# A graph layer whose loads move to ScalarE, with other buffers for gathered rows and sums

## The chip, the cores and the metric

The kernel runs on one core of a Trainium2 chip. The metric is the device time of one execution, in microseconds (us). PE is TensorE's matmul and PEld its weight load, DVE is VectorE, ACT ScalarE, POOL GpSimd and SP SyncE, which does no arithmetic and issues DMAs here. Each engine works through its own instructions in order; between engines, semaphores say when data is there or a buffer is free.

## What is computed

A layer of a graph network: 50,000 nodes of 160 features (64 scalars and 32 vectors of 3), 1,650,000 edges sorted by their destination `dst`, four numbers on each edge. For each edge the features of its source node are multiplied with the edge's numbers and with small weights; the results are summed over the edges of each destination; two more weights, a relu, the residual and a layer norm follow.

```python
e0, e1 = sh[:, 0:1], sh[:, 1:4]
dot  = einsum('eui,ei->eu', v[src], e1)
out0 = C0 * (s[src] * e0 @ W1 + dot * INV3 @ W2)
p3 = (s[src] @ W3)[:, :, None] * e1[:, None, :] * INV3
p4 = einsum('eui,uw->ewi', v[src] * e0[:, :, None], W4) * INV3
p5 = einsum('eui,uw->ewi', cross(v[src], e1[:, None, :]), W5) * INV6
out1 = C1 * (p3 + p4 + p5)
m_agg = segment_sum(concatenate([out0, out1]), dst)
h = concatenate([m_agg_s @ Ws * LIN_S, einsum('nui,uw->nwi', m_agg_v, Wv) * LIN_V])
x2 = x + relu(h)
result = layernorm(x + x2)
```

All of the weights are linear in the node's features, so the kernel sums first and multiplies after: for each of the four numbers k of an edge it sums (number k) × (source row of x) over the edges of a node, and multiplies the four sums of a node with matrices made of the weights.

## The kernel before

**Groups and pairs.** Edges are taken in units of 128, six units to a group (G = 6), two groups to a pair (PG = 2), twenty groups to a stretch of the tables (SG = 20, ten pairs). A group's destinations lie within a window of W = 32 nodes. There are 1,044 pairs, and 12,522 units.

**One pair.** `gather` (L345) issues twelve indirect DMAs on POOL (L349), each of 128 rows of x of 640 bytes, into one tile `xg` of [128, 12, 160] from a pool of four buffers. `spread` (L354) builds on DVE `hot`, which says for each edge which of the 32 nodes is its destination (L358), and `ha`, the same times the four numbers of the edge (L361). `group_sums` (L381) has PE multiply each unit's `ha` (128 edges × 4·32) with its gathered rows and sum the six units of a group in PSUM, in a tile `ps` of two groups from two buffers (L386; a matmul of float32 shows as two records). `turn_sums` (L394) has DVE transpose the pair's sums (L398) and add them into `ring` (L405) at a place that a register holds (`find`, L298).

**The order of the work.** The loop at L853 writes the order of all engines but POOL by hand: for pair p it asks for the gathers, then goes through the twelve units; after unit 1 comes the turning of pair p−1, after unit 3 the spreading of pair p+1, and after each unit `work(1.0)` (L748) takes tasks that are due, and a share of the steps of a pack. Tasks become due a number of pairs after or before some pair (`after_pair`, L741):

- of each block of 128 nodes whose last edges lie in pair p: `do_ahead` at p, which loads `xt` (the nodes' rows of x) for two blocks (L644); `do_block` at p+2, five matmuls of `ring` with the weights into `phb` (L704), then on DVE `y` and its statistics (L182 to L186); `do_root` at p+3, a square root on ACT (L191); `do_store` at p+4, L195 and L196 on DVE; `do_send` at p+6, the store of `o` (L784);
- of each stretch: `load` (L250) one stretch ahead; `cast` and `place` (L312), in which PE waits for `first` (L318) of DVE at L320, DVE makes the gathers' indices `si` and the places `rel`, and PE turns the edges' numbers into `pk` (L331);
- `ask_own` (L661) and `set_own` (L686), which bring in each node's own edge with two loads, `xr` and `sr`.

**Packs.** The edges of a node to itself lie among the others in the input. Sixteen packs (L463) take them out: a pack reads 128 rows of 790 edges (`read`, L471), copies and marks them (`begin`, ACT, L482 to L502), shifts the rest together with DVE (L559 to L566) and stores every row to `edges` and `selves` in HBM at an address that SP loads into a register (`store` and `put`, L594 to L619). It is a list of 77 steps, which the loop spreads evenly over the pairs that the pack has. The 17 store steps, of 16 DMAs each, follow each other.

**Queues.** `dq` (L247) is SP: the loads of `load`, of `read`, `xt`, `xr` and `sr`, the results and the packs' stores all stand in its one order. POOL has the gathers. ACT has the roots and the packs' copies.

**PSUM.** Eight banks: `bank` 1, `pk` 2, `marks` 1, `ps` 2, `phb` and the weights' products 2.

`wrote` (L374) tells the planner that a matmul needs no wait for the matmul that wrote the same buffer before, since that one's reader has been waited for.

Of the kernel before, what the change touches and what calls it, by code (L numbers as in the profile page):

```python
# [39 lines left out]
F32 = mybir.dt.float32  # L40
# [7 lines left out]
PSUM = bass.MemoryType.PSUM  # L48
# [54 lines left out]
def tile_gnn_resnorm(ctx: ExitStack, tc: tile.TileContext, x, src, dst, attr, W1, W2, W3, W4, W5, Ws, Wv, out, n_edges):  # L103
# [121 lines left out]
    last_of = [max(g for g in range(NG) if low[g] < (b + 1) * P) for b in range(nblocks)]  # L225

    with tc.tile_pool(name="once", bufs=1) as once, tc.tile_pool(name="raw", bufs=2) as rawp, \
            tc.tile_pool(name="idx", bufs=2) as idxp, tc.tile_pool(name="rows", bufs=4) as rowp, \
            tc.tile_pool(name="ops", bufs=3) as op, tc.tile_pool(name="sums", bufs=3) as sump, \
            tc.tile_pool(name="ring", bufs=2) as ringp, tc.tile_pool(name="node", bufs=3) as np_, \  # L230
            tc.tile_pool(name="ahead", bufs=4) as aheadp, tc.tile_pool(name="outs", bufs=3) as outp, \
            tc.tile_pool(name="psC", bufs=1, space=PSUM) as psC, tc.tile_pool(name="psK", bufs=2, space=PSUM) as psK, \
            tc.tile_pool(name="psP", bufs=1, space=PSUM) as psP, tc.tile_pool(name="psA", bufs=2, space=PSUM) as psA, \
            tc.tile_pool(name="psM", bufs=2, space=PSUM) as psM, ExitStack() as later_pools:

        spotp, ownp = (later_pools.enter_context(tc.tile_pool(name=name, bufs=bufs))
                       for name, bufs in (("spot", 3), ("own", 2)))
# [6 lines left out]
        slotsP = bank[:, 0, :]  # L244
        nc.vector.tensor_copy(slotsP, slots)

        dq = nc.sync  # L247
        begun = []

        def load(s):  # L250

            g0 = s * SG
            n = (min(NG, g0 + SG) - g0) * G
            if g0 >= NH:
                p0 = g0 * G * P - EH
                r6 = rawp.tile([P, P, 2 + NK], F32, name="r6")
                dq.dma_start(r6[:n].rearrange("u p c -> u (p c)"),
                             edges[0, p0 * (2 + NK):(p0 + n * P) * (2 + NK)].rearrange("(u q) -> u q", u=n))
                return s, n, None, r6[:n, :, 0], r6[:n, :, 1], r6[:n, :, 2:]
            e = slice(g0 * G * P, (g0 * G + n) * P)  # L260
            ri = rawp.tile([P, 2, P], I32, name="ri")
            ra = rawp.tile([P, P, NK], F32, name="ra")
            dq.dma_start(ri[:n, 0, :], src1[e].rearrange("(u p) o -> u (p o)", p=P))
            dq.dma_start(ri[:n, 1, :], dst1[e].rearrange("(u p) o -> u (p o)", p=P))
            dq.dma_start(ra[:n].rearrange("u p k -> u (p k)"), attr[e].rearrange("(u p) k -> u (p k)", p=P))
            return s, n, ri, None, None, ra[:n]

        def cast(loaded):
# [75 lines left out]

        def gather(placed, u, n):  # L345

            xg = rowp.tile([P, PG * G, D], F32, name="xg")
            for j in range(n):
                nc.gpsimd.indirect_dma_start(  # L349
                    out=xg[:, j, :], out_offset=None, in_=x,  # L350
                    in_offset=bass.IndirectOffsetOnAxis(ap=placed[0][:, u + j:u + j + 1], axis=0))
            return [xg[:, j, :] for j in range(n)]

        def spread(placed, u, n):  # L354

# [15 lines left out]
        def fresh(kind):  # L371
            written[kind].append([])

        def wrote(kind, ins):  # L374
            ws = written[kind]
            for old in ws[-3] if len(ws) > 2 else []:
                tc.declare_no_dep(ins.ins, old, reason="its reader has waited for it")
            ws[-1].append(ins.ins)
            return ins
# [83 lines left out]
        def pack(c):  # L463
# [7 lines left out]
            def read():  # L471
                T["pri"] = pri = packp.tile([P, 2, L + 1], I32, name="pri")
                T["pra"] = pra = packp.tile([P, LW, NK], F32, name="pra")
                dq.dma_start(pri[:n, 0, :L], src1[e].rearrange("(r e) o -> r (e o)", e=L))
                dq.dma_start(pri[:n, 1, :L], dst1[e].rearrange("(r e) o -> r (e o)", e=L))

                dq.dma_start(pri[:n, 1, L:], dst1[e0 + L:e0 + L + n * L].rearrange("(r e) o -> r (e o)", e=L)[:, 0:1])
                dq.dma_start(pra[:n, :L].rearrange("r e k -> r (e k)"), attr[e].rearrange("(r e) k -> r (e k)", e=L))

            def begin():  # L480
                T["prow"] = rows = packp.tile([P, L + 1, C], F32, name="prow")
# [142 lines left out]


            for head, j in [(False, j) for j in range(RS)] + [(True, 0)]:
                steps.append(partial(store, head, j))
            return steps + [stored]

        def rows_of(b):  # L630
# [8 lines left out]
        def ahead(bs):  # L639

            nb = rows_of(bs[0])[0]
            n0, n1 = rows_of(bs[0])[1].start, rows_of(bs[-1])[1].stop
            xt = aheadp.tile([P, BP, D], F32, name="xt")
            dq.dma_start(xt[:nb, :len(bs)], x[n0:n1, :].rearrange("(h n) d -> n h d", h=len(bs)))  # L644

            return [(xt[:, h],) for h in range(len(bs))]

# [13 lines left out]
        def ask_own(k, bs, got):  # L661

            n0, n1 = rows_of(bs[0])[1].start, rows_of(bs[-1])[1].stop
            assert rows_stored[0] == NR or row_start(rows_stored[0])[1][0] >= n1
            n = n1 - n0
            nq = next(q for q in range(math.ceil(n / W), n + 1) if n % q == 0)
            m = n // nq
            assert nq <= BP * P // W
            xr = ownp.tile([P, BP * P // W, D], F32, name="xr")
            sr = ownp.tile([P, BP * P // W], F32, name="sr")  # L670
            xs = x[n0:n1, :].rearrange("(w q) d -> w (q d)", q=nq).unsqueeze(0).to_broadcast([NK, m, nq * D])
            ss = selves[0, n0 * NK:n1 * NK].rearrange("(w q k) -> k w q", q=nq, k=NK)
            with nc.allow_non_contiguous_dma(reason="one number of each node"):
                if m == W:
                    dq.dma_start(xr[:, :nq].rearrange("p q d -> p (q d)"), xs)
                    dq.dma_start(sr[:, :nq], ss)
                else:
                    nc.vector.memset(xr[:, :nq], 0.0)
                    nc.vector.memset(sr[:, :nq], 0.0)
                    for k_ in range(NK):  # L680
                        r = slice(k_ * W, k_ * W + m)
                        dq.dma_start(xr[r, :nq].rearrange("p q d -> p (q d)"), xs[k_])
                        dq.dma_start(sr[r, :nq], ss[k_])
            got.extend((xr, sr, nq))

        def set_own(k, bs, got):  # L686
# [8 lines left out]
            if c0 + nq * W < c1:  # L695
                nc.vector.memset(ring[k][:, :, c0 + nq * W:c1], 0.0)

        def block(b, xt):
            nb, row = rows_of(b)
            k, c0 = b // SB, b % SB * P  # L700
            ph = psM.tile([P, D], F32, name="phb", tag="misc")
            fresh("misc")
            for i in range(ND):
                wrote("misc", nc.tensor.matmul(ph[:nb], ring[k][:, i, c0:c0 + nb], BWk[:, i, :],  # L704
                                               start=i == 0, stop=i == ND - 1))
                yield 1
            return norm1(np_, ph[:nb], xt[:nb], nb)
# [33 lines left out]
        def after_pair(p, f, *args):  # L741
            later.setdefault(p, []).append((f, args))
# [15 lines left out]
                else:  # L758
                    credit[0] -= cost

        of_nodes, resid, rstds, outs = {}, {}, {}, {}

        def do_ahead(b):
            bs = together(b)
# [1 line left out]
                of_nodes.update(zip(bs, ahead(bs)))  # L766

        def do_block(b):
            resid[b] = yield from block(b, *of_nodes.pop(b))

        def do_root(b):
            rstds[b] = norm2(np_, resid[b][1], rows_of(b)[0])
# [7 lines left out]
        def do_send(b):  # L780
            bs = together(b)
            if b == bs[-1]:
                n0, n1 = rows_of(bs[0])[1].start, rows_of(b)[1].stop
                dq.dma_start(out[n0:n1, :].rearrange("(h n) d -> n h d", h=len(bs)),  # L784
                             outs.pop(bs[0])[:rows_of(b)[0], :len(bs)])

        def do_cast(s):
# [57 lines left out]
                after_pair(p - 2, set_own, k, bs, got)  # L845
        for b, g in enumerate(last_of):
            p = g // PG
            after_pair(max(p, START - 1), do_ahead, b)
            for d, f in ((2, do_block), (3, do_root), (4, do_store), (6, do_send)):
                after_pair(p + d, f, b)  # L850
        later_pools.enter_context(tc.manual_schedule(engines={ET.SP, ET.PE, ET.DVE, ET.Activation}))
        turning = None
        for p, (s, g, ng) in enumerate(pairs):  # L853
# [8 lines left out]
                    after_pair(p + 8, read_flags)  # L862
            rows = gather(placed[s], (g - s * SG) * G, ng * G)
            for j, ps in enumerate(group_sums(p, rows, has.pop(p))):
                if j == 1 and turning:
                    turn_sums(*turning)
                    turning = None
                if j == 3 and p + 1 < len(pairs):
                    s1, g1, ng1 = pairs[p + 1]
                    has[p + 1] = spread(placed[s1], (g1 - s1 * SG) * G, ng1 * G)  # L870
                work(1.0)
                if packs and p >= START:
                    when = p + (j + 1) / (ng * G)
                    todo = math.ceil(len(packs[0]) * min(1, (when - began) / max(1, due[0] - began)))
                    for step in packs[0][done:todo]:
                        if step:
                            step()
                    done = max(done, todo)
                    if done == len(packs[0]):
                        packs.pop(0), due.pop(0)  # L880
                        done, began = 0, when
# [174 lines left out]
```

## Time and profile before

| | before |
|---|---|
| median of 3 runs | 17,993.06 us (17,989.49 to 18,003.85) |
| profiled execution | 18,022.17 us, span 18,020.0 us |
| mean granted TensorE clock | 0.625 |
| gathers | 12,522, of 0.949 us (median) |
| PE L386 | 25,044 records, 6,255 us |
| DVE `ha` L361 | 1,044 of 1.753 us, 1,830 us |
| SP stores of packs (L618) | 1,994 of 18.5 KB, 1,992 of 0.5 KB and 250 smaller |
| loads of `xt` / `xr` / results | 195 of 160 KB / 187 of 640 KB / 195 of 160 KB |
| moved by DMA | 1,337 MB, of these 1,027 MB by the gathers; 74 GB/s |

In a group's line of the page, "| busy, mean ns of one | idle before" follow the count. In a view of waits a line reads: who <- for whom: us in total, times, longest us; "issue" means that nothing in the profile ended the wait, "remote" that a semaphore did whose writer is not known. In an order of time a line begins with the start and the length in us, and the idle time of the engine before the instruction stands in brackets. A DMA that SP or ACT issues stands as SPq or ACTq, and its length is that of the issue.

### The profile page before, as it was taken

The page shows a single profiled execution, that of the slowest core. Times are in us where ns is not written, and L with a number is a line of the kernel's source. Part 1 is how long each engine was busy: PE and PEld are TensorE (multiplying, and loading weights), DVE is VectorE, ACT ScalarE, POOL GpSimd, SP SyncE. Part 2 cuts the span into 40 slices and gives each one's busy share as a digit, 9 for nine tenths or more (in the row PEclk, how much of TensorE's full clock was granted, in tenths as well). Part 3 has the DMA queues.
Part 4 walks back from the last instruction along what each step waited for, and adds up shares of the span by engine and source line. Part 5 has one row for each costly group of instructions (what it writes and reads, how often), then busy time and mean ns, then how long its engine had stood idle before and what let it go on. Part 6 is the DMA issues. An engine that isn't in the chain of part 4 may idle for free. (4 is left out here: it accounts for less than half of the span.)

```text
span 18020.0 us, 99721 instructions
## 1 busy us (share of the span) xinstructions
PE 6879.0 (38%) x29811; PEld 6014.7 (33%) x29812; DVE 7032.6 (39%) x11269; ACT 227.8 (1%) x479; POOL 12137.8 (67%) x12535
## 2 busy tenths in 40 slices
PE   3333334343333333333333333334333333333333
PEld 3333333333333333333333333333333333333333
DVE  4343443434434343443433434344343433434332
ACT  0000000000000000000000000000000000000000
POOL 6666666666666666666666666666666666666666
PEclk6666666666666666666666666666666666666666
DMA  2222323232232322323223232322323223232222
GB/s 71 74 69 72 80 71 81 69 82 72 73 79 70 83 71 73 79 69 81 72 72 79 70 79 72 82 69 72 80 70 82 69 73 80 69 79 72 73 72 63
DMA packets 961715, 1337.18 MB, mean 74 GB/s; under 512 B 411739, under 2 KB 716048, under 8 KB 957182
## 3 DMA queue, kind: packets, MB, share of 16 engines
q0 software_dynamic: 601056, 1026.60, 23.7%
q1 hardware_dynamic: 358674, 302.87, 6.1%
q8 instruction: 238, 3.90, 0.1%
q14 instruction: 307, 2.51, 0.0%
q10 hardware_dynamic: 1440, 1.29, 0.0%
HBM read 1258.50 MB, written 71.40 MB: 74 GB/s over the span
## 5 line engine op out<-in xcount | busy, mean ns | idle before, releaser
L349 POOL DMA_INDIRECT xg<-in_x,si x12522 | 12134.1, 969 | 5859.5 <-issue 3666.1
L386 PE MATMUL ps<-xg,ha 128*128 128x160 f32 x25044 | 6255.4, 383 | 9081.8 <-issue 8146.9
L386 PEld LDWEIGHTS ps<-xg,ha 128*128 128x128 f32 x25044 | 5171.1, 254 | 9859.0 <-issue 8902.6
L398 DVE STREAM_TRANSPOSE sums<-ps 128x320 f32<-128x320 f32 x1044 | 529.7, 507 | 6341.5 <-remote 4050.5
L361 DVE TENSOR_TENSOR ha<-hot,pk 128x1536 f32<-128x1536 f32 x1044 | 1830.2, 1753 | 35.8
L182 DVE SCALAR_TENSOR_TENSOR y<-phb,xt 128x160 f32<-128x160 f32 x391 | 125.6, 321 | 3508.3 <-PE ps L386 1623.2
L704 PE MATMUL phb<-BWk,ring 128*128 128x160 f32 (+1 forms) x3910 | 1181.7, 388 | 454.0 <-issue 452.9
L704 PEld LDWEIGHTS phb<-BWk,ring 128*128 128x128 f32 (+1 forms) x3910 | 925.6, 266 | 470.0 <-issue 469.5
L405 DVE TENSOR_TENSOR ring<-ring,sums 128x160 f32 x2087 | 683.1, 327 | 309.7 <-issue 224.2
L358 DVE TENSOR_TENSOR hot<-bank,rel 128x384 f32<-128x384 f32 x1044 | 572.4, 548 | 107.0 <-remote 70.5
L693 DVE STREAM_TRANSPOSE ring<-xr 128x1280 f32<-128x1280 f32 x188 | 466.1, 2479 | 6.5
L566 DVE COPY_PREDICATED prow<-marks,prow 128x2370 f32<-128x2370 int32 (+8 forms) x160 | 445.4, 2784 | 1.1
L320 PE MATMUL bank<-first,ones 120*128 120x20 f32 (+1 forms) x210 | 59.4, 365 | 815.1 <-DVE first L318 573.0
L320 PEld LDWEIGHTS bank<-first,ones 120*128 120x128 f32 (+1 forms) x210 | 49.8, 292 | 853.6 <-DVE first L318 597.5
L191 ACT ACTIVATE rstd<-mv,eps_t 128x1 f32<-128x1 f32 x391 | 115.2, 295 | 17061.4 <-DVE st L184 5415.1
L326 PE MATMUL bank<-ident,r 120*128 120x120 f32 x100 | 46.2, 462 | 703.1 <-issue 361.0
L566 DVE COPY_PREDICATED pra<-marks,pra 128x1580 f32<-128x1580 int32 (+8 forms) x160 | 306.5, 1915 | 0.0
L689 DVE TENSOR_TENSOR xr<-xr,sr 128x1280 f32<-128x1280 f32 x188 | 277.0, 1473 | 57.4 <-DMA sr<-selves 35.9
L326 PEld LDWEIGHTS bank<-ident,r 120*128 120x128 f32 x100 | 21.1, 211 | 727.4 <-issue 369.7
L196 DVE TENSOR_SCALAR o<-y,mv,rstd 128x160 f32<-128x160 f32 x391 | 146.1, 374 | 19.6 <-issue 3.7
L402 DVE TENSOR_TENSOR ring<-ring 128x1280 f32<-128x1280 f32 x97 | 143.0, 1474 | 1.8
L331 PE MATMUL pk<-ident,r 120*128 120x120 f32 (+1 forms) x400 | 139.5, 400 | 0.0
(349 smaller groups left out, 2156.2 us busy)
## 6 DMA issues: line engine op xcount, KB each, us to landing
xg<-in_x,si POOLq DMA_INDIRECT x12522
xr<-in_x SPq DMA_DIRECT2D x187, 640.0 KB
edges<-prow SPq DMA_DIRECT2D x1994, 18.5 KB
r<-edges SPq DMA_DIRECT2D x99, 360.0 KB
selves<-mine SPq DMA_DIRECT2D x1992, 0.5 KB
xt<-in_x SPq DMA_DIRECT2D x195, 160.0 KB
out<-o SPq DMA_DIRECT2D x195, 160.0 KB
pra<-in_attr SPq DMA_DIRECT2D x15, 1580.0 KB
```

Source lines behind the costliest of these rows:

```text
L196: nc.vector.tensor_scalar(o[:n], y[:n], mv[:n, 0:1], rstd[:n], op0=ALU.subtract, op1=ALU.mult)
L349: nc.gpsimd.indirect_dma_start(out=xg[:, j, :], out_offset=None, in_=x, in_offset=bass.IndirectOffsetOnAxis(ap=placed[0][:, u + j:u + j + ...
L358: nc.vector.tensor_tensor(hot[:, :n], slotsP[:, 0:W].unsqueeze(1).to_broadcast([P, n, W]), rel[:, u:u + n].unsqueeze(2).to_broadcast([P, n ...
L361: nc.vector.tensor_tensor(ha[:, :n], hot[:, :n].unsqueeze(2).to_broadcast([P, n, NK, W]), pk[:, :, u:u + n].rearrange("p k u -> p u k").un ...
L386: mm = nc.tensor.matmul(ps[:, j // G, :], ha[:, j].rearrange("p k w -> p (k w)"), xr, start=j % G == 0, stop=j % G == G - 1)
L398: nc.vector.transpose(at[:, :ng], ps[:, :ng].rearrange("p g (b f) -> p g b f", f=FB))
L402: nc.vector.tensor_tensor(ring[k][:, :, :TW - S], ring[k][:, :, :TW - S], ring[k - 1][:, :, S:], op=ALU.add)
L405: nc.vector.tensor_tensor(here, here, at[:, i], op=ALU.add)
L566: nc.vector.copy_predicated(what[:n, a:e], mi[:, r].unsqueeze(2).to_broadcast([n, e - a, what.shape[2]]), what[:n, a + d:e + d])
L689: nc.vector.tensor_tensor(xr[:, :nq], xr[:, :nq], sr[:, :nq].unsqueeze(2).to_broadcast([P, nq, D]), op=ALU.mult)
L693: nc.vector.transpose(ring[k][:, :, c0:c0 + nq * W].rearrange("p b (w q) -> p q b w", q=nq), xr[:, :nq].rearrange("p q (b f) -> p q b f", ...
L704: wrote("misc", nc.tensor.matmul(ph[:nb], ring[k][:, i, c0:c0 + nb], BWk[:, i, :], start=i == 0, stop=i == ND - 1))
```

## The change

- `loads` is ACT's queue. The loads of all stretches but the first, of the packs, `xt`, `xr` and `sr` and the stores of the results go through it; SP keeps the first stretch, the row table and the packs' stores.
- `do_ahead` comes three pairs earlier.
- Each store step of a pack is followed by two empty steps: 111 steps, not 77.
- Gathered rows lie in eight tiles of one group in place of four of two.
- `spread` of pair p+1 comes after unit 0, so before the turning of p−1.
- `ps` has three buffers; `phb` and the products have one, and `phb` holds the two blocks whose `xt` is loaded together. `wrote` looks back one buffer further for `ps` and no longer for the others.

```diff
-  rows: bufs=4            psA: bufs=2   psM: bufs=2
+  rows: bufs=4 * PG       psA: bufs=3   psM: bufs=1
-        dq = nc.sync
+        dq, loads = nc.sync, nc.scalar
...
         def load(s):
+            q = loads if s else dq
...
         def gather(placed, u, n):
-            xg = rowp.tile([P, PG * G, D], F32, name="xg")
+            rows = []
             for j in range(n):
+                if j % G == 0:
+                    xg = rowp.tile([P, G, D], F32, name="xg")
                 nc.gpsimd.indirect_dma_start(
-                    out=xg[:, j, :], out_offset=None, in_=x,
+                    out=xg[:, j % G, :], out_offset=None, in_=x,
...
         def wrote(kind, ins):
-            for old in ws[-3] if len(ws) > 2 else []:
+            for old in ws[-4] if kind == "ps" and len(ws) > 3 else []:
...
-                dq.dma_start(pri[:n, 0, :L], ...)
+                loads.dma_start(pri[:n, 0, :L], ...)
...
-                steps.append(partial(store, head, j))
+                steps += [partial(store, head, j), None, None]
...
-            dq.dma_start(xt[:nb, :len(bs)], ...)
+            loads.dma_start(xt[:nb, :len(bs)], ...)
...
-                    dq.dma_start(xr[:, :nq].rearrange("p q d -> p (q d)"), xs)
-                    dq.dma_start(sr[:, :nq], ss)
+                    loads.dma_start(xr[:, :nq].rearrange("p q d -> p (q d)"), xs)
+                    loads.dma_start(sr[:, :nq], ss)
...
-        def block(b, xt):
+        def block(b, xt, ph):
-            ph = psM.tile([P, D], F32, name="phb", tag="misc")
-            fresh("misc")
...
         def do_block(b):
-            resid[b] = yield from block(b, *of_nodes.pop(b))
+            bs = together(b)
+            if b == bs[0]:
+                sums_of[b] = psM.tile([P, BP, D], F32, name="phb", tag="misc")
+                fresh("misc")
+            resid[b] = yield from block(b, *of_nodes.pop(b), sums_of[bs[0]][:, b - bs[0]])
...
-                dq.dma_start(out[n0:n1, :].rearrange("(h n) d -> n h d", h=len(bs)),
+                loads.dma_start(out[n0:n1, :].rearrange("(h n) d -> n h d", h=len(bs)),
...
-            after_pair(max(p, START - 1), do_ahead, b)
+            after_pair(max(p - 3, START - 1), do_ahead, b)
...
             for j, ps in enumerate(group_sums(p, rows, has.pop(p))):
+                if j == 0 and p + 1 < len(pairs):
+                    s1, g1, ng1 = pairs[p + 1]
+                    has[p + 1] = spread(placed[s1], (g1 - s1 * SG) * G, ng1 * G)
                 if j == 1 and turning:
                     turn_sums(*turning)
                     turning = None
-                if j == 3 and p + 1 < len(pairs):
-                    s1, g1, ng1 = pairs[p + 1]
-                    has[p + 1] = spread(placed[s1], (g1 - s1 * SG) * G, ng1 * G)
```

More of the change, by code (lines that the diff above doesn't have):

```diff
@@ L227, in tile_gnn_resnorm @@
     with tc.tile_pool(name="once", bufs=1) as once, tc.tile_pool(name="raw", bufs=2) as rawp, \
-            tc.tile_pool(name="idx", bufs=2) as idxp, tc.tile_pool(name="rows", bufs=4) as rowp, \
+            tc.tile_pool(name="idx", bufs=2) as idxp, tc.tile_pool(name="rows", bufs=4 * PG) as rowp, \
             tc.tile_pool(name="ops", bufs=3) as op, tc.tile_pool(name="sums", bufs=3) as sump, \
@@ L232, in tile_gnn_resnorm @@
             tc.tile_pool(name="psC", bufs=1, space=PSUM) as psC, tc.tile_pool(name="psK", bufs=2, space=PSUM) as psK, \
-            tc.tile_pool(name="psP", bufs=1, space=PSUM) as psP, tc.tile_pool(name="psA", bufs=2, space=PSUM) as psA, \
-            tc.tile_pool(name="psM", bufs=2, space=PSUM) as psM, ExitStack() as later_pools:
+            tc.tile_pool(name="psP", bufs=1, space=PSUM) as psP, tc.tile_pool(name="psA", bufs=3, space=PSUM) as psA, \
+            tc.tile_pool(name="psM", bufs=1, space=PSUM) as psM, ExitStack() as later_pools:
         spotp, ownp = (later_pools.enter_context(tc.tile_pool(name=name, bufs=bufs))
@@ L256, in load @@
                 r6 = rawp.tile([P, P, 2 + NK], F32, name="r6")
-                dq.dma_start(r6[:n].rearrange("u p c -> u (p c)"),
+                q.dma_start(r6[:n].rearrange("u p c -> u (p c)"),
                              edges[0, p0 * (2 + NK):(p0 + n * P) * (2 + NK)].rearrange("(u q) -> u q", u=n))
@@ L262, in load @@
             ra = rawp.tile([P, P, NK], F32, name="ra")
-            dq.dma_start(ri[:n, 0, :], src1[e].rearrange("(u p) o -> u (p o)", p=P))
-            dq.dma_start(ri[:n, 1, :], dst1[e].rearrange("(u p) o -> u (p o)", p=P))
-            dq.dma_start(ra[:n].rearrange("u p k -> u (p k)"), attr[e].rearrange("(u p) k -> u (p k)", p=P))
+            q.dma_start(ri[:n, 0, :], src1[e].rearrange("(u p) o -> u (p o)", p=P))
+            q.dma_start(ri[:n, 1, :], dst1[e].rearrange("(u p) o -> u (p o)", p=P))
+            q.dma_start(ra[:n].rearrange("u p k -> u (p k)"), attr[e].rearrange("(u p) k -> u (p k)", p=P))
             return s, n, ri, None, None, ra[:n]
@@ L345, in gather @@
         def gather(placed, u, n):
-            xg = rowp.tile([P, PG * G, D], F32, name="xg")
+            rows = []
             for j in range(n):
+                if j % G == 0:
+                    xg = rowp.tile([P, G, D], F32, name="xg")
                 nc.gpsimd.indirect_dma_start(
-                    out=xg[:, j, :], out_offset=None, in_=x,
+                    out=xg[:, j % G, :], out_offset=None, in_=x,
                     in_offset=bass.IndirectOffsetOnAxis(ap=placed[0][:, u + j:u + j + 1], axis=0))
-            return [xg[:, j, :] for j in range(n)]
+                rows.append(xg[:, j % G, :])
+            return rows
         def spread(placed, u, n):
@@ L473, in read @@
                 T["pra"] = pra = packp.tile([P, LW, NK], F32, name="pra")
[L474 to L478, printed above, removed]
+                loads.dma_start(pri[:n, 0, :L], src1[e].rearrange("(r e) o -> r (e o)", e=L))
+                loads.dma_start(pri[:n, 1, :L], dst1[e].rearrange("(r e) o -> r (e o)", e=L))
+                loads.dma_start(pri[:n, 1, L:], dst1[e0 + L:e0 + L + n * L].rearrange("(r e) o -> r (e o)", e=L)[:, 0:1])
+                loads.dma_start(pra[:n, :L].rearrange("r e k -> r (e k)"), attr[e].rearrange("(r e) k -> r (e k)", e=L))
             def begin():
@@ L643, in ahead @@
             xt = aheadp.tile([P, BP, D], F32, name="xt")
-            dq.dma_start(xt[:nb, :len(bs)], x[n0:n1, :].rearrange("(h n) d -> n h d", h=len(bs)))
+            loads.dma_start(xt[:nb, :len(bs)], x[n0:n1, :].rearrange("(h n) d -> n h d", h=len(bs)))
             return [(xt[:, h],) for h in range(len(bs))]
@@ L681, in ask_own @@
                         r = slice(k_ * W, k_ * W + m)
-                        dq.dma_start(xr[r, :nq].rearrange("p q d -> p (q d)"), xs[k_])
-                        dq.dma_start(sr[r, :nq], ss[k_])
+                        loads.dma_start(xr[r, :nq].rearrange("p q d -> p (q d)"), xs[k_])
+                        loads.dma_start(sr[r, :nq], ss[k_])
             got.extend((xr, sr, nq))
@@ L759, in work @@
                     credit[0] -= cost
-        of_nodes, resid, rstds, outs = {}, {}, {}, {}
+        of_nodes, resid, rstds, outs, sums_of = {}, {}, {}, {}, {}
         def do_ahead(b):
```

## The prediction

> **What bounds the kernel now.** I read the busy table first, then the waits of POOL, then stretches of POOL between its pauses, then the order of time inside one stretch, and last the longest waits of DVE.
>
> ```profile
> span 18020.0 us, 99721 instructions
> PE 6879.0 (38%) x29811; PEld 6014.7 (33%) x29812; DVE 7032.6 (39%) x11269; ACT 227.8 (1%) x479; POOL 12137.8 (67%) x12535
> ...
> L349 POOL DMA_INDIRECT xg<-in_x,si x12522 | 12134.1, 969 | 5859.5 <-issue 3666.1
> ...
> POOL xg L349 <- issue: 3666.1, 11991, 2.1
> POOL xg L349 <- PE ps L386: 1224.7, 236, 46.9
> POOL xg L349 <- remote: 875.2, 223, 7.0
> ```
>
> No engine is full. POOL, which issues the 12,522 gathers of L349, is nearest: 12,134 us busy and 3,666 us of a fixed 0.30 us between two gathers. The other 2,193 us are pauses in which it waits for a buffer of `xg`, that is, for PE. Tempting reading: remove the pauses and end near 15,830. The next view speaks against it. Its rows are stretches from one resumption of POOL to another (start:end, length, POOL busy, gathers; one gather on an edge may be counted twice).
>
> ```profile
> 9023.39:9074.53 51.14, 34.15 (x37) 0.60 0.26 65
> ...
> 9194.10:9245.20 51.10, 34.15 (x36) 0.60 0.26 66
> 9245.20:9279.50 34.30, 22.80 (x25) 0.65 0.27 71
> 9279.50:9313.90 34.40, 23.72 (x24) 0.60 0.26 66
> ...
> 13203.90:13223.00 19.10, 12.17 (x13) 0.50 0.21 52
> ```
>
> POOL alone needs 1.255 us per gather (0.95 + 0.30). Yet 36 gathers take 51.1 us and 24 take 34.35, however many matmuls fall into the stretch, and the pause grows with the stretch: about 6 us after 36, 4.3 after 24. The difference of 12 gathers is 16.8 us, so something serves gathers at **1.40 us each**, and a stretch costs 1.40 per gather plus 51.1 − 50.4 = 0.7 us. What this server is I can't name from the profile. What it does is visible:
>
> ```profile
> 9016.56 0.95 POOL L349 DMA_INDIRECT xg<-in_x,si  x1 [0.30 <-issue]
> 9017.28 0.43 PE L386 MATMUL ps<-xg,ha 128*128 128x160 f32 x1 [2.37 <-issue]
> ...
> 9020.78 4.07 PE L386 MATMUL ps<-xg,ha 128*128 128x160 f32 x9 [0.97 <-issue]
> ...
> 9022.19 0.33 DVE L182 SCALAR_TENSOR_TENSOR y<-phb,xt 128x160 f32<-128x160 f32 x1 [30.06 <-PE ps L386]
> ...
> 9023.39 0.95 POOL L349 DMA_INDIRECT xg<-in_x,si  x1 [5.89 <-PE ps L386]
> ```
>
> While POOL runs ahead of the server, PE takes a step only every 1.4 us (2.8 between matmuls) with its rows long landed, and DVE waits 30 us for matmuls that were issued before 8,991. When POOL has paused for some 5 us, PE runs nine in 4 us, DVE and POOL are released together. The pause is how the lag of the server is paid, not a missing buffer. The last view shows waits that are not of this kind:
>
> ```profile
> 808.35 0.23 SPq L618 DMA_DIRECT2D edges<-prow  x1
> 808.68 0.23 SPq L618 DMA_DIRECT2D selves<-mine  x1
> 808.96 0.41 SPq L644 DMA_DIRECT2D xt<-in_x  x1
> ...
> 811.27 0.33 DVE L182 SCALAR_TENSOR_TENSOR y<-phb,xt 128x160 f32<-128x160 f32 x1 [93.08 <-DMA xt<-in_x]
> ...
> DVE y L182 <- DMA xt<-in_x: 241.7, 7, 93.1
> ```
>
> SP issues the row stores of a pack (L618, 272 of them, here from 522.1 to 808.68) in front of a load of `xt` that DVE needs; DVE stood 93 us, and POOL 46.9.
>
> **The sum of before.** 12,522 × 1.40 = 17,531. I count 423 pauses over 1 us; × 0.7 = 296. Start before the first gather 8, end after the last one 23. That leaves 162 of the 18,020. Four pauses of 46.9, 20.9, 19.6 and 12.9 us lie above the line of their neighbours by 42, 16, 17 and 11 = 86; the first three follow a late `xt` (DVE stood 93, 54 and 47 us), the fourth a pack whose edges were read late behind the same stores. Eight pauses of 9 to 12 us, most at the last pair of ten, carry about 5 each, 42 together: there PE stands before L320, which needs `first` of DVE, which stands behind `y`. Some 34 stay unplaced. The profiled run took 18,022, the median is 17,993: I carry −29.
>
> The page Perfetto Trace Analysis of the Trainium skill, section GPSIMD Engine Instruction, says not to trust a POOL instruction's span but its start-to-start spacing. By the span, gathers are 12,134 us; by the spacing of 1.255, 15,715; the stretches here say that neither sets the end.
>
> **The change, part by part.**
>
> Loads and results to ACT, and `xt` asked for three pairs earlier. About 930 issues leave SP (196 `xt`, 196 `out`, 374 of `xr`/`sr`, 100 `r6`, 64 of packs), and SP keeps 4,236 stores. The stores get two empty steps each: a pack goes from 77 steps to 111 over the same 61 pairs or so (some 1,040 us), the store part from 17/77 = 230 us to 51/111 = 478 us. SP needed 287 us for them at 522 to 808, more than 230, less than 478: its lag goes. `xt` now has 5 pairs, 85 us, before use. Gain: the four long pauses, −86; bounds 0 (the lateness moves to ACT) and −86. I take −86.
>
> ACT pays 930 issues at 0.41 to 0.45 us, about 400 us beside 228 busy: hidden in 17,000 us of idleness. But ACT is in order: L191, the root that DVE's L195 waits for, now stands behind loads, and in the built program each such issue also waits for the previous user of its completion semaphore, for 67 of the 196 `xt` a store of SP. A step of 16 stores took SP 287/17 = 17 us. A hold of that length is covered: DVE stood 28 to 35 us many times with an ordinary pause after it, and only above that did POOL pay. Cost 0; without the cover see the third rival.
>
> `ha` ahead of turning, three buffers `ps`. Same 1,044 × (0.55 + 1.75) us of DVE. In the built program PE at pair p waits for its own pair p−2 before and p−3 after, and `ha` of p+1 stands behind the turning of p−2, not p−1. PE may go one pair further before it hangs on a late release. The slow stepping itself stays, since the server causes it. For the eight pauses at L320 that extra pair is worth something between 0 and all of the 42; I take −20.
>
> `xg` in eight buffers of one group. The depth stays 48 gathers; POOL waits for six matmuls of pair p−4, not twelve, and twice as often (some 2,083 waits for PE against 1,045; each satisfied one hides in the 0.30 us). The pause stays proportional, 0.145 per gather; what shrinks is the 0.7 per stretch, if stretches lengthen. Now 12,522/423 = 29.6 gathers. Half a pair more would give 35.6, 352 stretches, −50; an upper bound of 40 gathers, 313, gives −77; if POOL just stops more often at half pairs, 26 gathers, 480, +40. I take −40, as PE's extra pair and the half pair both point that way.
>
> `phb` of two blocks in one buffer (psM 1): PE could wait for `y` of the block before, 2.7 pairs older than its own; the wait for p−3 covers nearly all. 0, bounds 0 and +15. Weights at the start share that one buffer: 0 to +10, within POOL's first 48 gathers.
>
> Sum: 18,020 − 86 − 20 − 40 = 17,874; −29 gives **17,845**. All upper gains: −86 − 42 − 77 − 34, less 29: 17,752. All gains at their least with +40, +25: 18,058.
>
> **The rivals.**
>
> 1. No server: the pauses are only lockstep of PE and DVE, and more decoupling dissolves them. For it: PE and DVE are idle 60%. Half of 2,193 gone: 16,900. Against: 36, 24 and 12 gathers lie on one line. Chance 0.06.
>
> 2. It doesn't do what it says: ACT takes over SP's lateness through the shared semaphores, stretches stay. −20 at most: about 17,985. For it: 371 of the 930 issues of ACT wait for a store of SP. Against: SP has 478 us for 287. Chance 0.13.
>
> 3. Slower: ACT in order. A load or `out` on ACT waits for SP, SP in turn waits on ACT (424 of its stores do), L191 is late, DVE stands at L195, and `ha` behind it. It decides from holds over 35 us. At two per pair of blocks in a store part (16 packs × 28 pairs / 5.3 = 84 places) costing 5 us in half of them, 42 × 5 = 210, less the gains kept, 60: 18,020 + 150 − 29 = 18,140. Against: 17 us a step. Chance 0.14.
>
> **How the numbers follow.** The likeliest case has 0.67; its own range is 17,752 to 17,957. For this kernel about 0.2% (36 us) can be told from none. Faster 0.67 + 0.06 = 0.73, same 0.13, slower 0.14. The range reaches into the second rival and leaves out the first and the third: 17,750 to 18,000.
>
> **What would show it.** Right: stretches of POOL still fit 1.40 per gather plus 0.7, now at lengths of 6 and not 12; POOL's waits beyond "issue" fall only to about 2,040 us; no wait for `xt`; no pause over 13 us; gathers still 0.95 us. Wrong in the server: 36 gathers in under 48 us. Wrong in SP's share: `xt` waits stay, or ACT's L191 holds DVE over 35 us. Wrong in the stretches: more than 450 pauses.

## The result: slower by 5.3%, and where the time went

The changed kernel takes 18,945 us (median of 4 runs, 18,921 to 18,964) against 17,995 for the kernel before: a ratio of 1.0527, 95% interval 1.0509 to 1.0545. The forecast was 17,845, its range ended at 18,000. It was wrong in sign.

The rows of the profile page after that answer to those shown of before (busy time and share of each engine; then groups: busy us and mean ns of one, idle time just before them and what ended most of it):

```profile
span 18949.8 us, 100810 instructions
...
PE 7176.6 (38%) x29811; PEld 6004.4 (32%) x29812; DVE 7041.1 (37%) x11269; ACT 224.6 (1%) x479; POOL 12120.2 (64%) x12535
...
L352 POOL DMA_INDIRECT xg<-in_x,si x12522 | 12116.5, 968 | 6808.3 <-issue 3605.2
...
L507 DVE TENSOR_TENSOR hit<-marks,prow 128x395 f32<-128x395 f32 (+1 forms) x32 | 26.9, 841 | 1130.0 <-ACT marks L506 1122.9
...
L195 DVE RECIPROCAL rstd<-rstd 128x1 f32<-128x1 f32 x391 | 60.9, 156 | 599.8 <-ACT rstd L191 558.4
```

PE is 298 us busier than before, at the same 38%; no other engine gained more than 9 us. POOL's gathers cost the same; its idle time grew by 949 us (5,859.5 to 6,808.3). DVE now loses 1,130 us at L507 and 600 at L195, nearly all of it waiting for ACT, an engine that is busy for 1% of the span. Before, nothing held it at L195, and its wait at the same marks (then L503) was:

```profile
DVE hit L503 <- ACT marks L502: 6.9, 3, 3.1
```

The view of waits of the run after (us in total, times, longest) says what ACT waits for:

```profile
POOL xg L352 <- issue: 3605.2, 11786, 1.8
...
POOL xg L352 <- PE ps L390: 2012.1, 278, 88.8
...
ACT prow L486 <- DMA edges<-prow: 1284.4, 13, 175.5
...
POOL xg L352 <- remote: 1136.2, 327, 10.6
DVE hit L507 <- ACT marks L506: 1122.9, 15, 122.2
...
ACT rstd L191 <- DMA edges<-prow: 804.2, 5, 184.5
```

ACT waits for SP's row stores: up to 175 us at a time at L486, where the next pack begins, and up to 185 at L191. POOL has 15 pauses of over 20 us, 1,170 us together, one at each of 15 packs; before it had two, 68 us. The rest kept its pace: stretches of 36 gathers between two pauses still take 1.40 us per gather plus 0.57, and `xt` no longer makes DVE wait at all. So the whole loss is in these 15 places: 1,102 us more of long pauses against 930 us more of span, the rest of the kernel being some 170 us faster. One of them, in the view of time (start, length, engine, line; "q" is the engine's queue, the bracket is the idle time before and what ended it):

```profile
4090.35 0.71 SPq L622 DMA_DIRECT2D edges<-prow  x1
...
4165.31 0.29 ACT L191 ACTIVATE rstd<-mv,eps_t 128x1 f32<-128x1 f32 x1 [21.99 <-DVE y L182]
4165.32 0.37 ACTq L648 DMA_DIRECT2D xt<-in_x  x1
...
4167.64 0.23 SPq L622 DMA_DIRECT2D selves<-mine  x1
...
4336.33 0.35 ACTq L258 DMA_DIRECT2D r<-edges  x1
...
4340.16 0.23 SPq L622 DMA_DIRECT2D selves<-mine  x1
4341.14 1.58 ACT L486 CAST prow<-pri 128x790 f32<-128x790 int32 x1 [175.53 <-DMA edges<-prow]
...
4347.44 0.84 DVE L507 TENSOR_TENSOR hit<-marks,prow 128x395 f32<-128x395 f32 x1 [105.80 <-ACT marks L506]
...
4359.86 0.95 POOL L352 DMA_INDIRECT xg<-in_x,si  x1 [80.77 <-PE ps L390]
```

Read it as two holds, one each way. SP stands from 4,091 to 4,168 and resumes just after ACT, released by DVE, issues its loads at 4,165 to 4,168. By then SP has issued only 51 of the pack's 272 stores in 584 us (it began at 3,582), and ACT is already through the read of the next pack. Now ACT stands: its load of `r` goes out at 4,336 and `begin` (L486), which overwrites `prow`, at 4,341, right after the last of the 221 stores that were left. DVE stood 106 us for it, POOL 81.

Why a store waits for a load: a DMA tells of its landing by a completion semaphore, and the build deals eight of them out to the DMAs of both queues. In the trace each of the eight is used by 522 to 538 DMAs of SP and 113 to 128 of ACT, and a DMA waits for the semaphore that it will use itself, until the last DMA on it has landed. For 424 of the 4,236 stores that last one is a DMA of ACT. The store that SP resumes with at 4,167.64 waits for the semaphore of the `xt` that ACT issued at 4,165.32. It is so at every long hold: SP stands over 20 us between two stores of a pack 84 times, 6,496 us together and up to 192 us at once, and each time the store that ends the hold has the semaphore that a DMA of ACT used last, issued 2 to 34 us before. In the pack shown 27 of the first 59 stores are tied so, then almost none: SP is held at the head of its burst and has the rest still to do when ACT comes round.

### The profile page after: what moved, and what is told of

Its sections match the earlier page's. It is cut to its first block, busy times and chain, and to the rows that moved or that the text cites. A ratio compares the mean times of both kernels' runs of the same rounds, so it can differ in the third digit from the quotient of the medians.

```text
span 18949.8 us, 100810 instructions
## 1 busy us (share of the span) xinstructions
PE 7176.6 (38%) x29811; PEld 6004.4 (32%) x29812; DVE 7041.1 (37%) x11269; ACT 224.6 (1%) x479; POOL 12120.2 (64%) x12535
## 5 line engine op out<-in xcount | busy, mean ns | idle before, releaser
L352 POOL DMA_INDIRECT xg<-in_x,si x12522 | 12116.5, 968 | 6808.3 <-issue 3605.2
L390 PE MATMUL ps<-xg,ha 128*128 128x160 f32 x25044 | 6380.4, 380 | 8961.5 <-issue 8272.5
L390 PEld LDWEIGHTS ps<-xg,ha 128*128 128x128 f32 x25044 | 5149.7, 250 | 9907.6 <-issue 9209.9
L706 PE MATMUL phb<-BWk,ring 128*128 128x160 f32 (+1 forms) x3910 | 1224.5, 383 | 1081.5 <-issue 1076.2
L507 DVE TENSOR_TENSOR hit<-marks,prow 128x395 f32<-128x395 f32 (+1 forms) x32 | 26.9, 841 | 1130.0 <-ACT marks L506 1122.9
L191 ACT ACTIVATE rstd<-mv,eps_t 128x1 f32<-128x1 f32 x391 | 115.2, 295 | 17182.0 <-DVE mv L186 9249.4
L195 DVE RECIPROCAL rstd<-rstd 128x1 f32<-128x1 f32 x391 | 60.9, 156 | 599.8 <-ACT rstd L191 558.4
```

What stands on the lines that cost most here:

```text
L352: nc.gpsimd.indirect_dma_start(out=xg[:, j % G, :], out_offset=None, in_=x, in_offset=bass.IndirectOffsetOnAxis(ap=placed[0][:, u + j:u + ...
L390: mm = nc.tensor.matmul(ps[:, j // G, :], ha[:, j].rearrange("p k w -> p (k w)"), xr, start=j % G == 0, stop=j % G == G - 1)
```

## The experiments

Each ratio is to the kernel before on the same chip, with its 95% interval. "Long pauses" are POOL's pauses of over 20 us. "Excess" is what POOL's stretches take above 1.40 us per gather, all summed; in each run 12,522 × 1.40 = 17,531 plus the excess plus the two ends (28 to 43 us) gives the span to within 5 us.

| run | ratio | interval | long pauses, us | excess, us |
|---|---|---|---|---|
| before | 1 | | 2, 68 | 462 |
| the change | 1.0527 | 1.0509–1.0545 | 15, 1,170 | 1,391 |
| e1 no empty steps | 1.0539 | 1.0521–1.0557 | 15, 1,130 | 1,385 |
| e2 loads on SP | 0.9925 | 0.9909–0.9942 | none | 297 |
| e3 before, empty steps | 0.9982 | 0.9972–0.9991 | none | 413 |
| e4 neither move nor empty steps | 0.9948 | 0.9932–0.9965 | 1, 42 | 336 |
| e5 `r6` on SP | 1.0396 | 1.0375–1.0417 | 27, 915 | 1,247 |
| e6 only `xt`, `out` on ACT | 1.0339 | 1.0321–1.0356 | 19, 627 | 1,137 |
| e7 before, queue move | 1.0571 | 1.0553–1.0589 | 15, 1,179 | 1,550 |
| e8 no root on ACT | 1.0415 | 1.0400–1.0431 | 15, 943 | 1,167 |
| e9 before, eight buffers | 0.9953 | 0.9938–0.9968 | 1, 31 | 339 |
| e10 before, `xt` earlier | 1.0002 | 0.9993–1.0011 | 2, 70 | 452 |
| e11 e2 with nine buffers | 0.9919 | 0.9906–0.9933 | none | 296 |
| e12 begin later | 1.0390 | 1.0373–1.0407 | 15, 912 | 1,227 |
| e13 e2, half the rows | 0.9918 | 0.9898–0.9938 | none | 386 |

### Which part costs: e1, e2, e3, e7

The empty steps out of the changed kernel (e1), into the kernel before (e3):

```
-                steps += [partial(store, head, j), None, None]
+                steps.append(partial(store, head, j))
```

> The changed kernel with one part undone: the stores of a pack follow each other in every step again, with no empty steps between them. Theory A (the two empty steps alone are the fault: they put the last store of a pack only 4 steps before the next pack's begin, SP is not done by then, and ACT, in order, stands at L486 until it is): the 15 jumps of 68 to 84 us vanish, ACT's waits at prow for the stores fall from 1284 us to under 150, DVE's wait for marks (1122.9 us) to under 150, and the time is 17,830 to 17,930. Theory B (the queue move alone is the fault: SP's stores wait for completion semaphores that ACT's DMAs used last, and ACT's DMAs for SP's): SP is still held, jumps of over 40 us remain at most packs, 18,450 to 18,950. Theory C (it takes both): as A here, and it parts from A in the next two runs.

> The kernel before with one part of the change alone: two empty steps after every store. Theory A: ACT stands at the begin of every pack, 18,650 to 19,050. Theory B and C: no jumps, and the burst of stores ahead of the xt loads is thinned, so the long pauses after a late xt (some 75 of the 86 us) may go: 17,900 to 18,000.

The queue move out (e2), and into the kernel before, alone (e7):

```
-        dq, loads = nc.sync, nc.scalar
+        dq, loads = nc.sync, nc.sync
```

> The changed kernel with the loads and results on SP again, everything else kept, the empty steps between stores too. Theory A: the stores still end 4 steps before begin, so jumps of about 70 us per pack remain, 18,600 to 18,950. Theory B: no wait of SP on ACT's DMAs, SP keeps its plan, jumps vanish, 17,850 to 18,000. Theory C: as B.

> The kernel before with one part of the change alone: loads and results on ACT, nothing else. If the move by itself carries the loss: the before's 17,994 plus 15 jumps of 65 to 75 us, less the 86 us of late xt, so 18,880 to 19,050. If the loss needs another part beside it (xt asked for earlier puts more loads between the stores): under 18,300.

All four say B, though e1 (18,964 us) and e7 (19,117 us, on a chip on which the kernel before took 18,098) end above the ranges that were set for it. Without the empty steps nothing changes (1.0539); with the loads back on SP all 15 pauses go, and the kernel is 0.75% faster than before; the move alone makes the kernel before 5.7% slower. The empty steps alone gain 0.18%: no long pause is left. The waits of e2 show the cure where the loss was:

```profile
POOL xg L352 <- PE ps L390: 818.0, 248, 9.6
...
DVE hit L507 <- ACT marks L506: 0.6, 1, 0.6
```

My first suspicion, theory A, that the empty steps put the last store too near the next `begin`, fell: in e1 SP had 243 stores of the same pack left when ACT came to the next read, with the steps 221.

### Which load ties the queues: e5, e6

e5 puts the loads of `r6` back on SP, by the first edit alone; e6 puts back all but `xt` and `out`:

```
-            q = loads if s else dq
+            q = dq
...
-                loads.dma_start(pri[:n, 0, :L], src1[e].rearrange("(r e) o -> r (e o)", e=L))
+                dq.dma_start(pri[:n, 0, :L], src1[e].rearrange("(r e) o -> r (e o)", e=L))
...
```

> The changed kernel with the 100 loads of r6 (and those of the start) back on SP, all other loads and results on ACT. Theory B1 (the shared completion semaphores: a store of SP waits until an ACT load that used its semaphore last is issued, so SP cannot run ahead, and some 240 of the 272 stores of a pack are left when ACT reaches the next pack): the ties by xt, out, xr and sr stay, SP still has over 150 stores left at the next pack's read, ACT stands at L486 for them, 18,500 to 18,950. Theory B2 (r6 reads the same DRAM tensor that the stores write, so on ACT it waits for all stores before it, and that is the hold): ACT's waits of 100 to 190 us vanish, 17,860 to 18,000.

> The changed kernel with only xt and out (392 issues) on ACT; r6, xr, sr and the reads of a pack are back on SP, behind its stores. In the built program a pack's stores are then tied to ACT some ten times, spread over the pack, where they were tied over 20 times, all within its first 40 stores. Theory B1 in its sharp form (what counts is where the ties lie: SP must not be held at the head of its burst): SP is held for short times, jumps under 20 us, 17,860 to 18,100. Theory B1 in its blunt form (any ACT load between SP's stores does it): jumps remain, 18,400 or more. Theory B2: 17,860 to 18,000, with no hold of SP over 60 us or so.

The time of e5, 1.0396, is that of B1, but its signs are mixed. At the next read 57 to 159 stores are left, over 150 in only three packs, and ACT's longest wait at L486 is 83 us, as B2 had it. The loss has moved: `r` now stands on SP behind held stores, and DVE waits for it:

```profile
DVE first L319 <- DMA r<-edges: 1506.7, 32, 82.8
```

So `r6`, which reads the tensor that the stores write, is a part of what held ACT, but not the cause. e6 settles it. With `xt` and `out` alone on ACT the ratio is still 1.0339, and here SP's tie to ACT cannot be one of data, as `xt` reads the input and `out` writes the output, which no store touches. Yet stores wait for both: of 86 holds of SP over 20 us between two stores, 82 (4,483 of 4,602 us) end with a store whose semaphore an `xt` or `out` used last. Two answers on the waits of e6, SP's queue first, then DVE:

```profile
SPq L622 <- DMA xt<-in_x: 282.2, 9, 72.5
...
SPq L622 <- DMA out<-o: 121.1, 18, 27.3
...
DVE xr L693 <- DMA sr<-selves: 1140.4, 41, 88.0
...
DVE first L319 <- DMA r<-edges: 592.4, 18, 53.0
```

So the blunt form holds, and my sharp form, that only ties at the head of the burst matter, fell: with ties spread over the pack, SP is held all the same, and the loads queued behind its stores (`sr`, `r`) are what DVE now waits for. The loss changes its place with the load that is left late. What was not tried is stores and loads on two queues with semaphores of their own.

### How the tie reaches DVE: e8, e12

e8 leaves L191 out of ACT; e12 gives `begin` 20 more empty steps:

```
-        rstd = pool.tile([P, 1], F32, name="rstd")
-        nc.scalar.activation(rstd[:n], mv[:n, 1:2], AF.Sqrt, bias=eps_t[:n])
-        return rstd
+        return mv[:, 1:2]
```

```
-            steps += [read, None, None, None, begin]
+            steps += [read] + [None] * 23 + [begin]
```

> The changed kernel without L191: the square root (and the small constant under it) is left out, and DVE's reciprocal reads the variance itself, so ACT's loads no longer stand behind an instruction that waits for DVE's statistics, and DVE waits for ACT only at the marks of a pack. It tells apart why ACT's loads come late to SP's stores. Theory P (ACT is in order and L191 keeps the loads behind DVE): the ties release early, SP has few stores left at the next pack's begin, jumps shrink to under 20 us each, 17,850 to 18,150. Theory Q (the loads' own waits, out for o, r6 for its buffer, xr for the ring, are as late as L191): SP is held as before, ACT still stands at L486 and marks come late, 18,450 to 18,950.

> The changed kernel with 20 more empty steps between the read of a pack and its begin (some 190 us of the plan), so that SP's stores have time to end before ACT comes to L486. Theory R (the loss passes through the begin alone: L486 waits for the stores, marks come late, DVE stops at L507): waits at L486 for stores go, jumps shrink to under 20 us, 17,900 to 18,200. Theory S (any load on ACT behind the ties passes it on: it waits for a store's semaphore, L191 behind it comes late, DVE stops at L195): the wait moves from L486 and L507 to L191 and L195, jumps of 50 to 80 us remain at most packs, 18,600 to 18,950.

Each takes away or eases one of ACT's two ways to DVE, and the loss goes by the other. In e8 (waits of DVE and SP; its lines are numbered two lower) DVE stands at the marks of a pack, and stores wait for `out`, which waits for DVE's own result:

```profile
DVE hit L505 <- ACT marks L504: 1518.7, 15, 114.7
...
SPq L620 <- DMA out<-o: 554.9, 7, 125.9
```

In e12 the marks cost nothing any more, and DVE stands at L195 for the root, which stands behind a load that waits for stores:

```profile
DVE rstd L195 <- ACT rstd L191: 1658.9, 16, 136.9
...
ACT rstd L191 <- DMA selves<-mine: 1106.8, 8, 185.4
...
ACT rstd L191 <- DMA edges<-prow: 1023.2, 6, 177.4
...
DVE hit L507 <- ACT marks L506: 1.7, 3, 0.6
```

Theories P and R fell, Q and S held: neither the root nor the `begin` is the cause, ACT as a whole is held. Each of the two gained something (the 15 pauses fell from 1,170 us to 943 and 912).

### What the other parts are worth: e4, e9, e10, e11

> The changed kernel with both the queue move and the empty steps undone: what is left is ha ahead of turning, xt asked for three pairs earlier, three ps buffers, one buffer for the block sums of two blocks, and xg in eight buffers of one group. By the terms of the prediction (ha and PE's extra pair -20, stretches -40, xt earlier up to -75 where 5 pairs cover SP's burst): 17,860 to 17,940 against 17,993. If POOL only stops more often at half pairs (+40): 18,000 to 18,040. Pauses over 1 us: about 352 if the stretches lengthen, 450 to 480 if they shorten.

> The kernel before with one part of the change alone: xg in eight buffers of one group, not four of two. Prediction's term: -40 (stretches lengthen from 29.6 gathers towards 36, the fixed 0.7 us of a stretch is paid less often) with +40 as the other end (POOL stops more often at half pairs). The changed kernel has 458 pauses, more than the 427 of before, so the stretches did not lengthen; if the fixed part of a stretch instead fell to about 0.5 us because POOL resumes half a pair earlier: 458 x 0.5 = 229 against 427 x 0.7 = 299, -70: ratio 0.996. If the fixed part stays 0.7: +20, ratio 1.001.

> The kernel before with one part of the change alone: xt asked for three pairs earlier, still on SP behind the stores. If the long pauses are due to a late xt and five pairs (85 us) cover SP's lag (93, 54 and 47 us were the longest stands of DVE): the stands at xt vanish, -60 to -75, ratio 0.996. If SP's lag is carried over (an earlier place in the same queue does not help, because SP is behind by more than that): 0 to -20, ratio 0.999 to 1.000.

> The second run's kernel (loads on SP, all else of the change) with nine buffers of xg in place of eight, all that the memory holds. If a stretch costs 1.40 us per gather plus a fixed part, a ninth buffer can lengthen stretches by up to 6 gathers at a pause: 27.3 to at most 30 gathers, 458 to 417 stretches, at 0.65 us up to -27: ratio to before 0.991 to 0.9925 where the second run had 0.9925. If pauses were for lack of buffers (no server), a ninth buffer would take more: below 0.985.

e4 is the changed kernel with the queue move and the empty steps undone; e9 and e10 put one part each into the kernel before (the diff is that of the change); e11 has `bufs=9` for `xg`. The eight buffers of one group are worth 0.47% by themselves, all that e4 has (0.52%): `ha` ahead of turning and the PSUM buffers add nothing that can be measured. `xt` three pairs earlier is worth nothing (1.0002), although DVE's wait for it fell from 241.7 us to 35.1. In its place the read of the next pack came late behind the same stores, and DVE stood at the marks. The waits of e10:

```profile
DVE y L182 <- DMA xt<-in_x: 35.1, 1, 35.1
...
DVE hit L503 <- ACT marks L502: 161.4, 3, 84.0
```

POOL's long pause in the first pack was 48.6 us, before 46.9. A ninth buffer (e11) brought no more than e2: the intervals lie over each other. By the count used here the pauses over 1 us are 423 before, 452 in the change, 450 in e2 and 449 in e4; the expectations of e9 and e11 put the first three at 427, 458 and 458.

### What the 1.40 us follow: e13

```
-                    out=xg[:, j % G, :], out_offset=None, in_=x,
+                    out=xg[:64, j % G, :], out_offset=None, in_=x,
```

> The second run's kernel (loads on SP) with each gather fetching 64 rows, not 128, and the matmul of L390 contracting over 64: half of the edges are left out of the sums, the number of gathers and matmuls stays. It asks what the 1.40 us per gather follow. If the server works row by row: 0.70 us per gather, POOL itself is then nearest, 12,522 x 1.255 = 15,715 and some 31 us at the ends, 15,750 to 16,300 (less if POOL's own 0.95 us shrink with the rows). If it works gather by gather: stretches keep 1.40 us per gather, 17,830 to 17,880.

Stretches between pauses of POOL (start:end, length, POOL busy and gathers, granted clock, DMA share, GB/s; one gather on an edge may be counted twice). First e9 with 36 and 24 gathers, then e2 with the same, then e13 with 24 and 30:

```profile
9031.02:9081.94 50.92, 34.14 (x36) 0.59 0.23 58
9133.82:9167.91 34.09, 22.75 (x25) 0.60 0.27 69
```

```profile
9114.43:9165.37 50.94, 34.16 (x36) 0.60 0.30 79
9165.37:9199.64 34.27, 22.81 (x25) 0.60 0.25 71
```

```profile
9019.08:9053.19 34.11, 21.73 (x25) 1.00 0.15 40
9165.71:9208.44 42.73, 27.18 (x30) 1.00 0.15 38
```

With half the rows and half the bytes 24 gathers still take 34.1 us and 30 take 42.7, 1.40 each plus 0.5 to 0.7, and the ratio is that of e2 (17,965 us, where the kernel before took 18,112 on the same chip). The pace follows the number of gathers, not their rows.

## Why the prediction was wrong, step by step

- **The sum of before.** It held. A stretch of 36 gathers costs 50.4 us plus a median of 0.55 to 0.96 in every kernel run here, from 0.8% faster to 5.7% slower than before, and the change left that alone. Rival 1 (no server) is out. A slip of 2 us is in the forecast: the −29 is the way from 18,022 to the median, but was taken off 18,020.
- **Loads and results to ACT: the step that failed.** I wrote "its lag goes" and took −86, because SP "keeps 4,236 stores" and the plan gave 478 us for 287 us of work, and I costed the in-order ACT at 0, because "a hold of that length is covered", from 17 us per step of 16 stores. Both rest on SP moving along its plan. I had read that 424 of its stores wait for ACT, and priced none of these waits. The runs show SP stopped at the head of the burst until ACT's loads are out, then ACT stopped until the burst is done: 165 to 244 us of remaining stores at a time (e1 and the change), not 17. e7 sizes the step: 19,117 − 18,098 = +1,019 us, where −86 was taken; the change against e2 gives 18,945 − 17,866 = +1,079. The price of ACT's issues was mis-sized too: not 930 at 0.41 to 0.45 us, about 400, but 2,411 us in the change, 1,295 of them in the 187 `xr`, which took 1,296 on SP before (the row `4342.44 10.96 ACTq L679 DMA_DIRECT2D xr<-in_x  x1` is one). What this adds to the loss is not shown.
- **Rival 3.** Its mechanism was the right one, in almost these words, with a chance of 0.14, but I had it in some 42 short places at 5 us (+210) where it sits in 15 long ones at 1,170 / 15 = 78 us of pause. It names DVE's stand at L195, which is the smaller part (558 us); the larger, 1,123 us, came at the marks of a pack, behind L486. The range stopped short of it: the holds were taken as covered, and ACT as idle. ACT sat idle for 17,182 us before its roots in the change too, and in that idle time it held DVE.
- **The empty steps, which I counted with the move.** They alone take the long pauses: 0.9982, excess 462 to 413 us, instead of −86 about −32 (0.18% of 18,003). For the long pauses themselves I named a late `xt`; e10 shows that an `xt` in time only hands the pause to the next load in the queue.
- **`ha` and three `ps`: −20.** Not shown; e4 and e9 differ by 0.05%, inside their intervals.
- **Eight buffers of one group: −40.** The sign was right, and the gain was twice the term: −0.47%, 85 us. The mechanism failed: stretches did not lengthen (474 in e9 against 423, 12,522 / 474 = 26.4 gathers and not 35.6), which I had said would mean a loss. What shrank is the fixed part: the mean excess of a stretch went from 462 / 423 = 1.09 to 339 / 474 = 0.71 us, the median of one of 36 gathers from 0.76 to 0.57. The eight pauses at L320 went with them: e9 has none over 10 us beside the one in the table.
- **What would show it.** Of my signs, 1.40 us, no `xt` wait and gathers at 0.95 us came true; POOL's waits of about 2,040 us and "no pause over 13 us" came near only in e2 (5,711 − 3,600 = 2,112 us, longest pause 9.7), which is the changed kernel without the queue move, at 17,866 us. That is near the 17,845 forecast, partly by chance, since its terms were off in both directions. Two of the signs of being wrong came true as well: DVE stood up to 119 us at L195 for L191, and there were 452 pauses.

The Trainium skill, page DMA: Bandwidth & Descriptors, section "Issuing engines are not separate DMA queues", says that starting DMAs from several engines saves only the sequencer time it takes to initiate them. The trace agrees that the move frees SP of issue time, 3,430 us of it before and 1,168 in e7; the kernel still lost 5.7%. The same page, section "Rules for kernel authors", advises to dedicate one semaphore to a DMA. Here eight are shared by two queues; the hold of SP for 77 us in the rows above is what that cost, and the 175 us of ACT after it is the wait for the stores that such holds had delayed.

The best version is the kernel of e2: all of the change but its queue move, 0.9925 of before (with a ninth buffer, e11, no different).

## What to carry to other kernels

Before moving DMAs to an idle engine, list what each of them and each DMA left behind will wait for in the built program; here a wait through a shared completion semaphore held a queue for up to 120 us with no data in common (e6), and two in-order queues that were tied both ways held each other in turn. Price such a hold by the longest piece of work that can stand between two ties (here some 220 stores, 170 us), not by the mean. Test the parts of a bundled change one by one: here a gain of 0.75% was hidden under a loss of 6%.

## What the runs showed of the hardware

The pace of 1.40 us per gather does not depend on rows (e13: 64 in place of 128), on bytes, or on the TensorE clock, whose granted mean rose from 0.62 in e2 to 1.00 in e13 with no gain in time (L390, which contracts over half the partitions there, took 482 ns on the mean, not 381). POOL's own gather fell only from 0.97 to 0.92 us on the mean. What serves gathers one by one at this pace stays open; nothing that was changed here moved it.

SP's row stores go slower while POOL gathers. In the change, two stores that follow each other within 6 us are issued 1.25 us apart in the median while POOL gathers, often 0.7, 1.4, 2.1 or 2.8, and 0.32 us apart while POOL pauses (start and length of each):

```profile
4187.03 0.70 SPq L622 DMA_DIRECT2D selves<-mine  x1
4189.83 0.70 SPq L622 DMA_DIRECT2D edges<-prow  x1
4191.93 0.70 SPq L622 DMA_DIRECT2D selves<-mine  x1
...
4300.53 0.23 SPq L622 DMA_DIRECT2D edges<-prow  x1
4300.86 0.23 SPq L622 DMA_DIRECT2D selves<-mine  x1
4301.18 0.23 SPq L622 DMA_DIRECT2D edges<-prow  x1
```

Of the 221 stores that were left at 4,168, SP issued 84 in the 111 us in which POOL still gathered, and 137 in the 61 us in which it stood. So a burst that is left late costs more while the gathers run; the reason is not shown.
